# First-layer output transposed as fp16 halves, and W1 in three bf16 parts

## The chip, the core and the metric

The kernel runs on one core of one Trainium2 chip. The time is that of the device for one execution, in microseconds (us), and the median over several executions is compared. A profile of one execution shows what each engine does: TensorE (PE in the profile, with weight loads as PEld), VectorE (DVE), ScalarE (ACT), GpSimd (POOL) and SyncE (SP). Matrix products land in PSUM, everything else lies in SBUF. Here GpSimd has two tasks: it does some additions, and it issues the DMA transfers that load the adjacency.

## What is computed

Two layers of a graph network on 4096 nodes with 64 features. The adjacency matrix is 4096 x 4096 of zeros and ones, held as float32.

```python
# layer 0: weights decay with the rank of a neighbour in its row
support = x @ W0
mask = (adj != 0)
rank = cumsum(mask, axis=1); deg = rank[:, -1:]
k = minimum(deg, 100); pos = rank - (deg - k)
w = mask * where(pos > 0, 0.5 ** (k - pos), 0)
x1 = layernorm(x + w @ support + b0)

# layer 1: mean over neighbours and the node itself
deg = clip(sum(adj, axis=1) + 1, 1)
h = (adj @ x1 + x1) / deg
z = concat([x1, h]) @ W1 + b1
z = relu(z); z = z / max(norm(z), 1e-12)
out = layernorm(x1 + z)
```

The change is in the part of layer 1 that doesn't need `adj @ x1`. Multiplied by deg, z becomes deg * (x1 @ W1a + b1) + x1 @ W1b + (adj @ x1) @ W1b, where W1a is the upper and W1b the lower half of W1. The kernel computes all but the last term ahead, and calls it c1. The factor deg drops out when z is divided by its norm.

## The kernel before

The transposed adjacency is cut into 8 slabs g of 512 target nodes (R), and each slab into 8 tiles k of 512 source nodes. A tile is loaded by one DMA from GpSimd's queue (`load_next`, L109), is cast from float32 to bf16 on the way, and takes one of 23 buffers. The 64 pairs (g, k) are the 64 steps of the main loop, in the order of slabs and, within a slab, from k = 7 down to 0. Six loads are issued ahead of the loop; step i then issues load number 6+i (counted from 0) after GpSimd's other work of that step.

A step has these parts, in TensorE's order: `count` (L237) counts the neighbours of tiles that come next, in groups that are called chunks (of one tile in slab 0, two in slabs 1 to 3, four after that). In the first step of a chunk of two or four, the tiles of the next chunk are counted in pairs, and in a chunk of four a second pair two steps later. `spread` (L255) turns the counts of a whole chunk into ranks. `weigh` (L270, L280) makes the exponents of the weights of this step's tile in two PSUM buffers, which ACT (L287) and DVE (L288) turn into weights w. `some_sums` (L307) does up to four early products of layer 1 with tiles that are still in SBUF. `gather` (L298) multiplies the weights of the step before with x.

A slab's first layer ends in the steps after its last tile. With i = 8(g+1), hooks put this work on each engine: i+1 the sum and the product with W0 (`first_hT`, `first_pz`), i+2 the addition of x and the moments, i+4 the normalized x1 (L422), i+5 its fp16 high half (`first_hi`, ACT, L427) and what that leaves (`first_xl`, DVE, L431), i+6 the low half (`first_lo`, ACT, L434), scaled by 2048. The halves stand side by side in x1hl. They are the stationary operand of all products adj @ x1.

c1 is made by a second line of work in the same steps. `first_px` (i+5, L439) transposes x1 in float32, four blocks of 128 nodes. `first_x1T` (i+6, ACT, L442) copies that to SBUF, over a row of ones. `first_pu` (i+6, L447) multiplies it by W1 in float32; the bias b1 is W1's 65th row. `first_c1` (i+8, DVE, L453 and L454) multiplies one half by deg and adds the other.

What fixes the order: each engine works through its own instructions as the program lists them. Within a step of the loop GpSimd's hooks come ahead of `load_next`, and DVE's hooks come at the end of the step. GpSimd's hooks in the loop are the split of x (`split_x`, slab 0 only), the load of x for a slab (`load_x`, at 8g+3) and the addition of b0 to it (`add_b0`, L227, at 8g+7). A load waits until the tile that had its buffer is no longer needed, that is until its sums are done or until ACT has copied it to fp8 (`keep_next`, L320), and until the transfer eight issues ahead of it in GpSimd's queue has landed. The PSUM buffers named "m" are two, and count, rank, transpose and product take turns in them. `ready` says from which step on a tile may be used for early sums: from the step in which the x1hl of its source nodes is written.

After the 64 steps a last stage, written out by hand, does the rest of adj @ x1 slab by slab (`own`), with the last slab's first layer between, and then the output.

Of the kernel before, what the change touches and what calls it, by code (L numbers as in the profile page):

```python
# [9 lines left out]
F32 = mybir.dt.float32  # L10
BF16 = mybir.dt.bfloat16
FP16 = mybir.dt.float16
# [4 lines left out]
ALU = mybir.AluOpType  # L17
AX = mybir.AxisListType
PE = mybir.EngineType.PE
ACT = mybir.EngineType.Activation  # L20
DVE = mybir.EngineType.DVE
POOL = mybir.EngineType.Pool
SP = mybir.EngineType.SP

P = 128
R = 512
TB = R // P
# [5 lines left out]
LO = 2048.0  # L33
# [7 lines left out]
def adj_resnorm_kernel(  # L41
# [26 lines left out]
    nc = tc.nc  # L68
    D = w0.shape[0]
    NG, NK = adjT.shape[0], adjT.shape[1]  # L70
# [5 lines left out]
    const = ctx.enter_context(tc.tile_pool(name="const", bufs=1))  # L76
# [8 lines left out]
    ps_m = ctx.enter_context(tc.tile_pool(name="ps_m", bufs=2, space=PSUM))  # L85
# [9 lines left out]
    when = {s: i for i, s in enumerate(steps)}  # L95
# [17 lines left out]
    x1 = const.tile([P, NB, D], F32, name="x1")  # L113
    xhl = const.tile([P, NB, 2 * D], FP16, name="xhl")
    x1hl = const.tile([P, NB, 2 * D], FP16, name="x1hl")
    c1 = const.tile([P, NB, D], F32, name="c1")
# [36 lines left out]
    ident = const.tile([P, P], F32, name="ident")  # L153
# [29 lines left out]

    w0_sb = const.tile([P, D], F32, name="w0_sb")
    wn_sb = const.tile([P, D], F32, name="wn_sb")
    w1_sb = const.tile([D + 1, 2 * D], F32, name="w1_sb")
    b0_sb = const.tile([P, D], F32, name="b0_sb")
    part = {}
    deg = const.tile([P, NB], F32, name="deg")
    least = const.tile([P, NB], F32, name="least")  # L190
    x1T = const.tile([D + 1, R], F32, name="x1T")
    nc.vector.memset(x1T[D : D + 1, :], 1.0)

    def load_weights():
        nc.sync.dma_start(out=w0_sb[0:D, :], in_=w0)
        nc.sync.dma_start(out=w0_sb[D:P, :], in_=w0)
        nc.sync.dma_start(out=b0_sb, in_=b0.partition_broadcast(P))
        nc.sync.dma_start(out=w1_sb[0:D, 0:D], in_=w1[0:D, :])
        nc.sync.dma_start(out=w1_sb[0:D, D : 2 * D], in_=w1[D : 2 * D, :])
        nc.sync.dma_start(out=w1_sb[D : D + 1, 0:D], in_=b1[None, :])  # L200
        nc.sync.dma_start(out=wn_sb[0:D, :], in_=w1[D : 2 * D, :])
        nc.sync.dma_start(out=wn_sb[D:P, :], in_=w1[D : 2 * D, :])

# [12 lines left out]
    def prepare():  # L216
        nc.vector.tensor_scalar(w0_sb[0:D, :], w0_sb[0:D, :], 2.0**W_EXP, None, ALU.mult)
        nc.vector.tensor_scalar(w0_sb[D:P, :], w0_sb[D:P, :], 2.0**W_EXP / LO, None, ALU.mult)
        nc.vector.memset(w1_sb[D : D + 1, D : 2 * D], 0.0)

    def prepare_last():
        nc.vector.tensor_scalar(wn_sb[D:P, :], wn_sb[D:P, :], 1.0 / LO, None, ALU.mult)

    def add_b0(g):

        xs = x1[:, ts(g, TB), :]
        nc.gpsimd.tensor_tensor(xs, xs, b0_sb.unsqueeze(1).to_broadcast([P, TB, D]), ALU.add)  # L227
# [78 lines left out]
    def second(acc, g, b, first, last):  # L306
        nc.tensor.matmul(acc, lhsT=x1hl[:, b, :], rhs=A[g][b // KB][:, b % KB, :], start=first, stop=last)  # L307
# [23 lines left out]

    def ready(i, g, b):
        k = b // KB
        return i >= NK * (k + 1) + 6 and i >= when[g, k]

    def evict_part(g):
        acc = acc1.pop(g)
# [6 lines left out]
    def some_sums(i, n):  # L344

        done = None
        while n and todo and done is None and ready(i, todo[0][0], todo[0][1]):
            g, b, first, last = todo.pop(0)
            if first:
                acc1[g] = ps_a.tile([P, R], F32, tag="acc1", name=f"acc_part_{g}_{b}")  # L350
            second(acc1[g], g, b, first, last)
            have[g] = b // KB + 1
            n -= 1
            if last:
                done = g
        return done


    ep = {}
# [74 lines left out]
        nc.scalar.mul(x1hl[:, ts(g, TB), D : 2 * D], ep["xl", g], LO)  # L434

    def first_px(g):
        px = ep["px", g] = ps_m.tile([D, R], F32, tag="m", name=f"px_{g}")
        for t in range(TB):
            nc.tensor.transpose(px[:, ts(t, P)], x1[:, g * TB + t, :], ident)  # L439

    def first_x1T(g):
        nc.scalar.copy(x1T[0:D, :], ep["px", g])  # L442

    def first_pu(g):
        pu = ep["pu", g] = ps_m.tile([P, TB, 2 * D], F32, tag="m", name=f"pu_{g}")
        for t in range(TB):
            nc.tensor.matmul(pu[:, t, :], lhsT=x1T[:, ts(t, P)], rhs=w1_sb, start=True, stop=True)  # L447

    def first_c1(g):

        pu = ep["pu", g]
        t1 = epi.tile([P, TB, D], F32, tag="sq", name=f"t1_{g}")
        nc.vector.tensor_tensor(t1, pu[:, :, 0:D], deg[:, ts(g, TB)].unsqueeze(2).to_broadcast([P, TB, D]), ALU.mult)  # L453
        nc.vector.tensor_tensor(c1[:, ts(g, TB), :], pu[:, :, D : 2 * D], t1, ALU.add)  # L454

    hooks = defaultdict(list)

    def at(i, engine, fn, *args):
        hooks[i, engine].append((fn, args))
# [5 lines left out]
    for k in range(NK):  # L465
        i = when[0, k]
        at(i, POOL, split_x, k)
        at(i, DVE, split_x_low, k)
    at(NK - 2, DVE, prepare)
    at(2 * NK + 2, DVE, prepare_last)  # L470
    for g in range(NG):
        at(NK * g + 3, POOL, load_x, g)
        at(NK * g + 7, POOL, add_b0, g)
    for g in range(NG - 1):
        i = NK * (g + 1)
        at(i + 1, ACT, first_hT, g)
        at(i + 1, PE, first_pz, g)

        at(i + 2, DVE, first_y, g)
        at(i + 2, DVE, first_mv, g)  # L480
        at(i + 3, "ACT, late", first_s, g)
        at(i + 4, DVE, first_r, g)
        at(i + 4, DVE, first_x1, g)
        at(i + 5, ACT, first_hi, g)
        at(i + 5, DVE, first_xl, g)
        at(i + 5, PE, first_px, g)
        at(i + 6, ACT, first_lo, g)
        at(i + 6, ACT, first_x1T, g)
        at(i + 6, PE, first_pu, g)
        at(i + 6, DVE, first_least, g)  # L490
        at(i + 8, DVE, first_c1, g)


# [9 lines left out]

    nc.vector.memset(w0_sb, 0.0)
    load_weights()
    spread(0, NK - 1)
    held = None
    for c, chunk in enumerate(chunks):
        ahead = chunks[c + 1] if c + 1 < len(chunks) else []
        n, m = len(chunk), len(ahead)  # L510
# [5 lines left out]
        for (g, k), share in zip(chunk, shares):  # L516
            i = when[g, k]
# [26 lines left out]
    L = NG - 1  # L544
# [3 lines left out]
    def own(g, b0, b1):  # L548

        for b in range(b0, b1):  # L550
            second(acc[g], g, b, b == have[g] * KB, b == NB - 1)
# [136 lines left out]
    first_least(L)  # L688
    own(5, 24, last)
    own(2, 16, last)  # L690
    first_px(L)
    first_x1T(L)
    own(0, 16, 24)
    own(5, last, NB)
    last_hT(5)
    own(2, last, NB)
    last_hT(2)
    first_pu(L)
    first_c1(L)

    u = unit(5, 2)
# [117 lines left out]
```

## Time and profile before

| | us |
|---|---|
| median of 3 executions | 272.93 |
| lowest and highest | 272.83, 273.19 |
| execution that was profiled | 273.33 |
| its span, from first to last instruction | 271.5 |

Some groups of the profile of this execution, in the work that the change touches. A float32 matmul appears as two passes in the trace where it has 128 rows or columns of products, so L447 has 64 records for 32 products.

| line, engine | what | count | mean ns of one |
|---|---|---|---|
| L439 PE | transpose of x1, float32, 128 columns | 32 | 273 |
| L447 PE | product with W1, float32, 128 columns | 64 | 275 |
| L442 ACT | copy of x1T, 64 x 512 | 8 | 567 |
| L453 DVE | deg times one half | 8 | 416 |
| L454 DVE | sum of both | 8 | 425 |
| L109 POOL | issue of a load of the adjacency | 65 | 548 |

A matmul's duration in the trace includes its way through the array; the distance from one start to the next is what TensorE's time is made of. It is 109 ns for L439 and 111 ns for L447.

How to read the profile: each engine has a share of busy time. For TensorE this says little of how near it is to its peak. The page also cuts the span in 40 slices and gives the busy share of each in tenths. The chain of waits follows back, from the last instruction, what each one waited for. A wait is shown behind an instruction in brackets: how long its engine stood idle, and what ended it.

### The profile page before, as it was taken

The page shows a single profiled execution, that of the slowest core. Times are in us where ns is not written, and L with a number is a line of the kernel's source. Part 1 is how long each engine was busy: PE and PEld are TensorE (multiplying, and loading weights), DVE is VectorE, ACT ScalarE, POOL GpSimd, SP SyncE. Part 2 cuts the span into 40 slices and gives each one's busy share as a digit, 9 for nine tenths or more (in the row PEclk, how much of TensorE's full clock was granted, in tenths as well). Part 3 has the DMA queues.
Part 4 walks back from the last instruction along what each step waited for, and adds up shares of the span by engine and source line. Part 5 has one row for each costly group of instructions (what it writes and reads, how often), then busy time and mean ns, then how long its engine had stood idle before and what let it go on. Part 6 is the DMA issues. An engine that isn't in the chain of part 4 may idle for free.

```text
span 271.5 us, 4838 instructions
## 1 busy us (share of the span) xinstructions
PE 237.3 (87%) x1865; PEld 105.0 (39%) x1865; DVE 176.3 (65%) x480; ACT 157.9 (58%) x226; POOL 61.9 (23%) x111
## 2 busy tenths in 40 slices
PE   8397688979899999999899999999998999997820
PEld 2122124334434343443344344434343546555710
DVE  5566634875596778367846684576577456597884
ACT  4456627897798869768854463436545322146351
POOL 8565551231101320322122121210200000221100
PEclk9979959999999999999999999999999999999985
DMA  6999999999997999799999999990500000010010
GB/s 97 195 230 234 241 212 214 222 214 214 223 214 141 165 211 214 124 171 214 182 179 205 203 162 180 168 168 12 98 2 0 0 2 0 0 42 20 19 58 21
DMA packets 12072, 37.13 MB, mean 137 GB/s; under 512 B 2066, under 2 KB 3218, under 8 KB 12050
## 3 DMA queue, kind: packets, MB, share of 16 engines
q0 software_dynamic: 10128, 35.66, 68.1%
q1 hardware_dynamic: 1922, 1.18, 1.5%
q8 instruction: 14, 0.23, 0.3%
q14 instruction: 8, 0.07, 0.1%
HBM read 69.34 MB, written 1.05 MB: 259 GB/s over the span
## 4 chain that ended last, share of the span: by engine, by line
PE 51%; DVE 11%; ACT 8%; issue 3%; POOL 1%; DVEq 0%; POOLq 0%; ACTq 0%
PE acc L298 10%; PE acc_part L307 9%; PE v L270 8%; PE v L280 5%; ACT w L287 4%; PE acc_right L307 3%; DVE w L288 3%; PE cnt L237 3%; PE vb L307 3%; PE pu L447 2%; PE va L307 2%; PE pz L594 2%; PE pz L395 2%; DVE x L422 1%; ACT a L320 1%
## 5 line engine op out<-in xcount | busy, mean ns | idle before, releaser
L288 DVE TENSOR_SCALAR w<-v 128x1024 int16<-128x1024 f32 x64 | 78.2, 1222 | 45.3 <-PE v L280 45.2
L287 ACT ACTIVATE w<-v,less 128x1024 int16<-128x1024 f32 x64 | 71.3, 1114 | 56.9 <-PE v L280 39.9
L298 PE MATMUL acc<-w,xhl 128*128 128x512 bf16 x256 | 67.2, 385 | 2.4 <-ACT hT L389 2.1
L109 POOL DMA_DIRECT2D a<-in_adjT_dram x65 | 35.5, 548 | 122.1 <-PE acc_part L307 49.9
L270 PE MATMUL v<-a,tri 64*64 64x512 bf16 x512 | 42.0, 397 | 4.3 <-ACT w L287 2.6
L298 PEld LDWEIGHTS <-xhl 128*128 128x128 f16 x256 | 23.9, 99 | 32.5 <-issue 9.5
L320 ACT CAST a<-a 128x1024 fp8e4<-128x1024 bf16 x32 | 33.3, 1039 | 0.0
L307 PEld LDWEIGHTS <-x1hl 128*128 128x128 f16 x224 | 19.8, 98 | 27.0 <-issue 5.7
L307 PE MATMUL acc_part<-a,x1hl 128*128 128x512 bf16 x108 | 28.0, 381 | 1.8 <-ACT x1hl L434 1.3
L247 DVE TENSOR_TENSOR cs<-cnt,cs 128x512 bf16<-128x512 f32 x20 | 13.8, 691 | 20.5 <-PE cnt L237 20.4
L237 PE MATMUL cnt<-a,pick 128*32 128x512 bf16 x256 | 21.9, 399 | 6.0 <-DMA a<-in_adjT_dram 6.0
L280 PE MATMUL v<-near,mine 32*128 32x512 bf16 x256 | 25.7, 391 | 0.2 <-ACT near L257 0.2
L270 PEld LDWEIGHTS <-tri 64*64 64x64 bf16 x512 | 12.6, 106 | 30.2 <-issue 28.0
L257 ACT ACTIVATE near<-rep,most 128x512 bf16<-128x512 f32 x28 | 19.1, 682 | 3.8 <-PE rep L255 3.7
L633 POOL TENSOR_TENSOR y<-y,x 128x256 f32<-128x256 f32 x7 | 5.0, 726 | 56.1 <-DVE y L630 56.1
L280 PEld LDWEIGHTS <-mine 32*128 32x128 bf16 x256 | 6.5, 91 | 24.9 <-issue 24.9
L255 PE MATMUL rep<-cs,further 128*128 128x512 bf16 x28 | 11.2, 400 | 3.7 <-DVE cs L247 1.7
L307 PE MATMUL acc_right<-a,x1hl 128*128 128x512 fp8e4 (+1 forms) x56 | 12.7, 379 | 0.0
L237 PEld LDWEIGHTS <-pick 128*32 128x32 bf16 x256 | 4.6, 94 | 19.8 <-issue 11.5
L655 ACT ACTIVATE o<-y,off,r_l 128x64 f32<-128x64 f32 x28 | 9.7, 428 | 3.1 <-issue 1.7
L382 DVE BATCH_NORM_STATS2 st_l<-y 128x6 f32<-128x64 f32 x60 | 9.0, 214 | 0.7 <-POOL y L633 0.6
L427 ACT CAST x1hl<-x 128x256 f16<-128x256 f32 x8 | 3.2, 406 | 10.1 <-DVE x L422 10.1
(139 smaller groups left out, 238.6 us busy)
## 6 DMA issues: line engine op xcount, KB each, us to landing
a<-in_adjT_dram POOLq DMA_DIRECT2D x63, 512.0 KB, 9.7
c<-in_x_pairs_dram POOLq DMA_DIRECT2D x8, 128.0 KB, 11.6
x<-in_x_dram POOLq DMA_DIRECT2D x8, 128.0 KB, 7.9
out_dram<-o SPq DMA_DIRECT2D x7, 128.0 KB, 1.7
a<-in_adjT_dram POOLq DMA_DIRECT2D x2, 256.0 KB, 4.7
out_dram<-o_7a SPq DMA_DIRECT2D x1, 64.0 KB, 1.9
out_dram<-o_7b SPq DMA_DIRECT2D x1, 64.0 KB, 1.5
w_sb<-in_L_gnn_weight_dram SPq DMA_DIRECT2D x2, 16.0 KB, 6.5
```

The source lines that it names most:

```text
L109: nc.gpsimd.dma_start(out=a[:, qs, :], in_=adjT[g, k][:, qs, :])
L237: nc.tensor.matmul(cnt[g][q * 32 : (q + 1) * 32, :], lhsT=pick[:, PW - 2 * k : PW - 2 * k + 32], rhs=A[g][k][:, q, :], start=first, stop=last,
L247: nc.vector.tensor_tensor(new, cnt[g], cs[g], ALU.add)
L255: nc.tensor.matmul(pr, lhsT=further, rhs=cs[g], start=True, stop=True)
L257: nc.scalar.activation(near[g], pr, AF.Relu, bias=most, scale=-1.0)
L270: nc.tensor.matmul(v[i][halves[c], r, :], lhsT=tri[halves[r], :], rhs=A[g][k][halves[r], 2 * i + c, :], start=True, stop=False,)
L280: nc.tensor.matmul(v[i][:, r, :], lhsT=mine[rows, 2 * k : 2 * k + 2, :], rhs=nr[rows, :], start=False, stop=True,)
L287: nc.scalar.activation(w[:, 0:2, :], v[0], AF.Relu, bias=less)
L288: nc.vector.tensor_scalar(w[:, 2:4, :], v[1], -STEP * MAX_NEIGH, 0.0, ALU.add, ALU.max)
L298: nc.tensor.matmul(acc0[g], lhsT=xhl[:, b, :], rhs=w[:, q, :].bitcast(BF16), start=(k, q) == (NK - 1, 0), stop=(k, q) == (0, KB - 1),)
L307: nc.tensor.matmul(acc, lhsT=x1hl[:, b, :], rhs=A[g][b // KB][:, b % KB, :], start=first, stop=last)
L320: nc.scalar.copy(kept[g, k][:, qs, :], A[g][k][:, qs, :], saturate=False)
```

## The change

x1 is no longer transposed in float32. The two fp16 halves in x1hl, 128 columns for each node, are transposed instead, so x1T is 128 x 512 in fp16: rows 0 to 63 the high half, rows 64 to 127 the low half times 2048. W1 stands twice below itself, the lower copy divided by 2048, so that one product takes both halves. W1 is cut into three bf16 parts whose sum is W1, and each block of nodes is multiplied by the three, into one sum in PSUM. The 65th row is gone; deg * b1 is now made by GpSimd (`first_b1`), which also adds it to the rest (in `first_c1`).

The steps move too. `first_px` goes from i+5 to i+6 and `first_x1T` and `first_pu` go from i+6 to i+7; early sums (`ready`) wait for one more step. `prepare_last`, with the making of the three parts, goes from step 18 to step 7. In the last stage four products of slab 0 come ahead of `first_px`.

```diff
-    w1_sb = const.tile([D + 1, 2 * D], F32, name="w1_sb")
+    w1_sb = const.tile([P, 2 * D], F32, name="w1_sb")
+    w1_parts = const.tile([P, 3, 2 * D], BF16, name="w1_parts")
+    b1_sb = const.tile([P, D], F32, name="b1_sb")
...
-    x1T = const.tile([D + 1, R], F32, name="x1T")
-    nc.vector.memset(x1T[D : D + 1, :], 1.0)
+    x1T = const.tile([P, R], FP16, name="x1T")
+    ident16 = const.tile([P, P], FP16, name="ident16")
+    nc.vector.tensor_copy(ident16, ident)
...
-        nc.sync.dma_start(out=w1_sb[0:D, 0:D], in_=w1[0:D, :])
-        nc.sync.dma_start(out=w1_sb[0:D, D : 2 * D], in_=w1[D : 2 * D, :])
-        nc.sync.dma_start(out=w1_sb[D : D + 1, 0:D], in_=b1[None, :])
+        for h in range(2):
+            for c in range(2):
+                nc.sync.dma_start(out=w1_sb[h * D : (h + 1) * D, c * D : (c + 1) * D], in_=w1[c * D : (c + 1) * D, :])
+        nc.sync.dma_start(out=b1_sb, in_=b1.partition_broadcast(P))
...
-        nc.vector.memset(w1_sb[D : D + 1, D : 2 * D], 0.0)
...
         nc.vector.tensor_scalar(wn_sb[D:P, :], wn_sb[D:P, :], 1.0 / LO, None, ALU.mult)
+        nc.vector.tensor_scalar(w1_sb[D:P, :], w1_sb[D:P, :], 1.0 / LO, None, ALU.mult)
+        for j in range(3):
+            nc.vector.tensor_copy(w1_parts[:, j, :], w1_sb)
+            if j < 2:
+                nc.vector.tensor_tensor(w1_sb, w1_sb, w1_parts[:, j, :], ALU.subtract)
...
-        return i >= NK * (k + 1) + 6 and i >= when[g, k]
+        return i >= NK * (k + 1) + 7 and i >= when[g, k]
...
-        px = ep["px", g] = ps_m.tile([D, R], F32, tag="m", name=f"px_{g}")
+        px = ep["px", g] = ps_m.tile([P, R], FP16, tag="m", name=f"px_{g}")
         for t in range(TB):
-            nc.tensor.transpose(px[:, ts(t, P)], x1[:, g * TB + t, :], ident)
+            nc.tensor.transpose(px[:, ts(t, P)], x1hl[:, g * TB + t, :], ident16)
...
-        nc.scalar.copy(x1T[0:D, :], ep["px", g])
+        nc.scalar.copy(x1T, ep["px", g])
...
-            nc.tensor.matmul(pu[:, t, :], lhsT=x1T[:, ts(t, P)], rhs=w1_sb, start=True, stop=True)
+            for j in range(3):
+                nc.tensor.matmul(
+                    pu[:, t, :], lhsT=x1T[:, ts(t, P)], rhs=w1_parts[:, j, :], start=j == 0, stop=j == 2
+                )
+
+    def first_b1(g):
+
+        nc.gpsimd.tensor_tensor(
+            c1[:, ts(g, TB), :],
+            deg[:, ts(g, TB)].unsqueeze(2).to_broadcast([P, TB, D]),
+            b1_sb.unsqueeze(1).to_broadcast([P, TB, D]),
+            ALU.mult,
+        )
...
-        nc.vector.tensor_tensor(c1[:, ts(g, TB), :], pu[:, :, D : 2 * D], t1, ALU.add)
+        nc.vector.tensor_tensor(t1, pu[:, :, D : 2 * D], t1, ALU.add)
+        nc.gpsimd.tensor_tensor(c, c, t1, ALU.add)
...
-    at(2 * NK + 2, DVE, prepare_last)
+    at(NK - 1, DVE, prepare_last)
...
-        at(i + 5, PE, first_px, g)
         at(i + 6, ACT, first_lo, g)
-        at(i + 6, ACT, first_x1T, g)
-        at(i + 6, PE, first_pu, g)
+        at(i + 6, PE, first_px, g)
         at(i + 6, DVE, first_least, g)
+        at(i + 7, POOL, first_b1, g)
+        at(i + 7, ACT, first_x1T, g)
+        at(i + 7, PE, first_pu, g)
         at(i + 8, DVE, first_c1, g)
...
     own(2, 16, last)
+    own(0, 16, 20)
     first_px(L)
+    first_b1(L)
     first_x1T(L)
-    own(0, 16, 24)
+    own(0, 20, 24)
```

The addition on GpSimd in `first_c1` is written in DVE's hook of step i+8, so in GpSimd's order it stands behind the load of step i+8 and ahead of that of step i+9.

## The prediction

> **What bounds the kernel now.** I read, in this order, busy shares and slices, the chain of waits, the sums of waits, and then the timelines of POOL, DVE and PE, because the change touches GpSimd, and GpSimd issues every load of the adjacency.
>
> ```profile
> PE 237.3 (87%) x1865; PEld 105.0 (39%) x1865; DVE 176.3 (65%) x480; ACT 157.9 (58%) x226; POOL 61.9 (23%) x111
> ...
> PEclk9979959999999999999999999999999999999985
> DMA  6999999999997999799999999990500000010010
> ```
>
> TensorE is the busiest engine, and the DMA engines are hardly less busy over the first 27 slices (about 183 us). Until about 40 us most counts of a tile start within 0.04 us of its landing; after that TensorE sets the pace. The chain shows this:
>
> ```profile
> 108.65 0.57 ACT x1T L442
> 109.22 0.04 issue
> 109.26 0.38 PE rep L255
> ...
> 159.03 0.44 PE px L439 x4
> ...
> 162.94 0.89 PE pu L447 x8
> ```
>
> The transposes (0.44 us a slab) and products (0.89) lie on the chain, and so, once, does the copy of x1T between them. Now GpSimd and the loads:
>
> ```profile
> 44.91 0.53 POOL L109 DMA_DIRECT2D a<-in_adjT_dram  x1 [1.91 <-DMA a<-in_adjT_dram]
> 52.46 0.72 POOL L227 TENSOR_TENSOR x<-x,b_sb 128x256 f32<-128x256 f32 x1 [7.02 <-DMA x<-in_x_dram]
> 53.13 2.17 POOL L109 DMA_DIRECT2D a<-in_adjT_dram  x4
> ...
> 108.72 0.53 POOL L109 DMA_DIRECT2D a<-in_adjT_dram  x1 [5.12 <-ACT a L320]
> ...
> 190.90 0.53 POOL L109 DMA_DIRECT2D a<-in_adjT_dram  x1 [11.30 <-PE acc_part L307]
> ```
>
> The reader is to see that GpSimd works strictly in order: an addition that waited 7.02 us for its data held four loads, which left at once when it was done. Number the tiles 0 to 63 in their order of loading; step i issues load 6+i. Load 39 is the issue at 108.72, load 63 the one at 190.90. The DMA view cut to that last issue, with nothing else under way, has its landing:
>
> ```profile
> a<-in_adjT_dram POOLq DMA_DIRECT2D x1, 512.0 KB, 5.0
> ```
>
> By the trace's semaphores loads 35, 39, 47, 55 and 63 land 3.1, 4.7, 6.5, 10.6 and 2.6 us ahead of their counting. That is all the cover there is. The timelines of DVE and PE around step 56:
>
> ```profile
> 193.40 1.22 DVE L288 TENSOR_SCALAR w<-v 128x1024 int16<-128x1024 f32 x1 [2.39 <-PE v L280]
> 194.54 0.41 DVE L453 TENSOR_TENSOR t<-pu,deg 128x256 f32<-128x256 f32 x1
> 194.99 0.42 DVE L454 TENSOR_TENSOR c<-pu,t 128x256 f32<-128x256 f32 x1
> ```
>
> ```profile
> 198.29 0.62 PE L237 MATMUL cnt<-a,pick 128*32 128x512 bf16 x8
> ```
>
> The c1 work of step 56 ends at 195.41. The last load is counted in the second half of that PE line, at 198.52.
>
> **What the Trainium skill says.** "TensorE: Matmul & The Clock Gate", Architectural detail, calls the GpSimd queue strict FIFO; the 7.02 us above agrees. "DMA: Bandwidth & Descriptors", Anatomy of one DMA (SWDGE path), gives 2.0 us fixed plus bytes over 436 GB/s. One MB read per tile makes that an estimate of 4.4 us; the trace has 5.0, which I use. TensorE, Part 1, says that the clock halves after a window of about 3.4 us without enough work. Here the clock fell after windows in which, by my count of the matmuls, TensorE streamed 9% and 27% of the time (until 13.5 and 34.0 us) and stayed after one of 39%. TensorE, Back-to-back issue gap, has 56 ns for 128 columns; the trace has 109 ns for 256 columns in bf16 (L555), half of which is 55, and 25 ns between matmuls that load 128x128 bf16 weights for one column (L397), so weight loads don't bind.
>
> **The change part by part.**
>
> Transposes and products: 4 x 109 ns = 0.44 and 8 passes x 111 = 0.89 us a slab go; 4 x 55 = 0.22 and 12 x 55 = 0.67 come. No 16-bit transpose and no bf16 product of 128 columns is in the trace; between the 25 and the 109 ns of the rows named, the 16 new ones take 0.4 to 1.7 us a slab, which is +0.9 of gain to -0.4 of loss a slab against 1.33; at 55, TensorE saves 0.44 us a slab, 3.5 in all, where it is the bound. The x1T copy keeps 512 columns (0.56).
>
> Moves by a step: px to i+6, x1T and pu to i+7, and most groups of early sums one step later (the bound 7 for 6). As many sums as before are done by the end. TensorE's waits for the low half go at 59.55 (0.30), 83.27 (0.52) and 133.71 (0.52), and those of rep for x1T at 109.26 (0.93) and 186.62 (0.14). In slabs 1, 3 and 6 the transposes stood just before a wait of TensorE for DVE's weights (81.64, 132.08, 208.63), so their removal only widens that wait. Where the transposes were hidden, the new ones (+0.22) and the shorter products (-0.22) cancel, and only a removed wait counts. So in slab 0 0.44 + 0.30 = 0.75 goes, in slab 1 0.5, in slab 2 0.44 + 0.93, in slab 3 0.5, in slab 4 0.6 (0.44 and part of the 0.32 wait for DVE's eviction at 151.16), in slab 5 0.55; in slab 6 I take 0.25, since w(63) on ACT is late next. In the tail px now needs the low half of slab 7, which ends at 221.71; four more sums carry TensorE from 219.94 to 220.80 only, so it waits 0.95 and the 0.44 is lost: +0.35 net.
>
> Start: w1_parts add about 1.3 us of DVE at step 7 (rows of 0.18 to 0.29 us), in a 1.77 us idle time before L247 at 40.46: nothing, or 0.3 if longer. The ident16 copy replaces a memset of 0.48 before a DMA-bound stretch: nothing. SP has one DMA issue more (w1 four times, b1 broadcast), some 255 packets; the hardware queue's 1922 packets took 1.5% of the span, so 0.5 us of the DMA engines' time while they are the bound. Between 0 and 0.6; I take 0.3.
>
> GpSimd: eight products (0.72 each, like L227) on a deg that is long there, nothing. Eight additions of t1 (0.72), and these wait for DVE's second c1 operation of step 8g+16, in the queue ahead of load 8g+23. Before, that load had no such wait: load 39 left at 108.72, in step 30, and now can't before step 32. DVE's order is w 1.15, t 0.45, c 0.42; then the addition 0.77 with its semaphore, the issue, and 5.0 us: the load lands 7.85 us after w(8g+16) starts. It is counted two steps later in slabs 2 to 5: 5.47, 5.62, 5.47 and 5.12 us after that w. So TensorE stops for 2.4, 2.2, 2.4 and 2.7 us. All of it is exposed, since the counts stand ahead of the weighing in TensorE's order.
>
> The loads behind follow at 2.45 us in a full queue and up to 3.8 after an empty one or beside a load of x; I take 2.9 for the next and 3.5 with x. In slab 2 load 41 then lands 6.4 after 39 and is due 5.33 after: 1.1 more (0.3 to 2.1). In slab 4, 0.2; slab 3, nothing. In slab 1 load 31 itself is in time, but 32 to 35, with x between, land by 19.2 us after w(24), and load 35 is due 16.85 after (16.5, plus a group of sums that now falls in between, 0.86, less the transposes): 2.35 (0.8 to 3.6). In slab 0 the margin is 0.9: nothing, or 0.5.
>
> The sum, as shifts against before, w(i) being the start of DVE's weights of step i. Start and slab 0: w(16) -0.45. Slab 1's 0.5 and the group of sums that moves behind w(24): -1.8, thus 88.75. Load 35 is counted 19.2 later, at 107.95 for 107.06: +0.9. Without the x1T wait (0.93) w(32) is at 0.0. Load 39 adds 2.4, load 41 1.1: +3.5. Slab 3's 0.5: +3.0; load 47: +5.2. Slab 4's 0.6: +4.6; loads 55 and 57: +7.2. Slab 5's 0.55: +6.65; load 63: +9.35. Slab 6 -0.25, small waits for w that the stops cover -0.2, tail +0.35: +9.25. That is 13.35 of stops less 4.1 of gains. The span of 271.5 becomes 280.8. The execution profiled took 273.33 with what lies around its span, so 282.6 for it; the median of the runs shown is 0.4 below: 282.2.
>
> **The rivals.**
>
> The hold is harmless: the change is then worth its gains alone, 4.1 less the 0.2 that only the stops cover, 273.33 - 3.9 - 0.4 = 269.0 us. For it: loads land 4 to 14 us early through most of the middle. Against: the holding load is exactly the one whose cover disappears, and the wait is in the program's order. This is the rival on the faster side; it decides if the stops of TensorE together stay below 3.9 us of the 13.35.
>
> The hold bites in part: landings 1 us quicker, or less TensorE work saved between w and the count, 272.5 to 277.5: 13.35 less some 7. Against: no load of 512 KB lands within less than 5.0 us.
>
> The clock joins in: a stop of 2.4 us wholly inside one window of 3.4 leaves some 26% work, about where the clock fell at 34.0. Each time costs a window at half speed, 1.7 us. One to four of these: 283.9 to 289. Against: a stop must fall wholly in one window, for about a third of the positions.
>
> **How the numbers follow.** The forecast, 277.5 to 285, has a chance of 0.62; the clock beyond that 0.14; the hold in part 0.12; the hold harmless 0.12. The range that leaves 2 in 10 out is 275 to 287.5; the likeliest case's own is 277.5 to 285. A difference under 0.2%, 0.5 us, can't be told from none here. Faster 0.13, same 0.02, slower 0.85.
>
> **What would show it.** Right: POOL's loads 39, 47, 55 and 63 directly after an addition that waited for DVE's t; TensorE's counts (and their weight loads) waiting for the adjacency some 2 to 3 us a slab from slab 1 on, in place of 6.0 us in all before and none after 40 us; px at 55 ns, pu at 55. Wrong: no waits of the counts for DMA after 50 us, or landings well under 5 us after such an issue, or time lost in DVE or ACT in place of this.

## The result, and the profile after

| | before | after |
|---|---|---|
| median, us | 273.06 | 291.26 |
| lowest and highest | 272.83, 273.31 | 291.1, 291.8 |
| ratio | | 1.067 [1.0651, 1.0688] |
| span of the profiled execution | 271.5 | 289.4 |
| mean granted TensorE clock | 0.965 | 0.942 |

The change makes the kernel 18.2 us slower. The page of the profile after, TensorE's and GpSimd's shares and the slices of the clock, the DMA engines and what they moved:

```profile
PE 237.6 (82%) x1866; PEld 103.2 (36%) x1897; DVE 178.1 (62%) x485; ACT 158.2 (55%) x226; POOL 72.3 (25%) x127
...
PEclk9989989999999995998998999989999999999985
DMA  6999999994998999079919991799240000000111
GB/s 105 192 231 236 230 215 215 220 216 67 188 213 161 167 211 212 10 146 206 214 36 164 201 213 25 127 198 216 60 93 0 0 2 0 2 5 32 36 38 36
```

Where the DMA line was an almost unbroken row of nines before, it now has holes: 67, 10, 36, 25 and 60 GB/s, one for each of five slabs, and from the second on some 29 us (four slices of 7.2) apart. Three of the clock's dips (slices 19, 22 and 27) come one or two slices after a hole; the deepest (slice 16) comes six after the first. The sums of waits, us in total, times, and the longest, first before and then after:

```profile
POOL a L109 <- PE acc_part L307: 49.9, 16, 11.3
...
PE cnt L237 <- DMA a<-in_adjT_dram: 6.0, 7, 2.7
```

```profile
POOL c L476 <- DVE t L475: 86.5, 7, 18.2
...
PE cnt L246 <- DMA a<-in_adjT_dram: 22.3, 14, 3.1
...
POOL a L109 <- PE acc_part L316: 13.6, 5, 5.8
```

GpSimd now spends up to 18.2 us in one wait, for DVE's part of c1. Its waits for a buffer behind early sums shrink from 49.9 us to 13.6: the addition that waits comes first. TensorE's counts wait 22.3 us for the adjacency in place of 6.0. The load that stands directly behind the waiting addition is called the held one below, and the wait itself the hold.

One slab in detail, slab 2. GpSimd's timeline, with load 39 as the first of the two at 123.37 (before: 108.72):

```profile
103.33 1.13 POOL L109 DMA_DIRECT2D a<-in_adjT_dram  x2
122.70 0.72 POOL L476 TENSOR_TENSOR c<-c,t 128x256 f32<-128x256 f32 x1 [18.24 <-DVE t L475]
123.37 1.10 POOL L109 DMA_DIRECT2D a<-in_adjT_dram  x2
124.46 0.56 POOL L123 DMA_DIRECT2D x<-in_x_dram  x1
124.99 2.14 POOL L109 DMA_DIRECT2D a<-in_adjT_dram  x4
```

The chain of waits through the same place (start, length, what):

```profile
120.53 1.23 DVE w L297
121.76 0.34 DVE t L474
...
122.12 0.44 DVE t L475
...
122.70 0.67 POOL c L476
123.37 5.09 DMA a<-in_adjT_dram
128.47 0.04 issue
128.51 0.40 PE cnt L246 x4
```

From DVE's weights to the count it is 7.98 us; before, TensorE came to this count 5.47 us after the same weights. The difference, 2.5 us, is about the 2.33 that TensorE then stands still (a stop), and it repeats. TensorE's timeline at the last load, which stands for the line at 198.29 shown of before:

```profile
213.47 0.40 PE L246 MATMUL cnt<-a,pick 128*32 128x512 bf16 x4
216.16 0.40 PE L246 MATMUL cnt<-a,pick 128*32 128x512 bf16 x4 [2.28 <-DMA a<-in_adjT_dram]
```

The two tiles of a pair were one group of eight matmuls; now the second waits 2.28 us for its landing. All stops after 45 us, by the load that was late: load 25 1.27, load 34 0.14, load 35 3.11, load 39 2.33, load 47 2.23, load 55 2.40, load 63 2.28. They sum to 13.76.

The clock is the second loss. TensorE's busy time in seven stretches, with the clock granted in each (start and end, length, busy, clock, DMA share, GB/s):

```profile
105.60:109.00 3.40, 1.59 (x15) 1.00 1.07 216
109.00:115.84 6.84, 5.17 (x32) 0.50 1.07 214
126.10:129.50 3.40, 1.07 (x20) 1.00 1.06 210
129.50:132.90 3.40, 3.18 (x11) 0.50 1.06 201
132.90:153.00 20.10, 18.74 (x166) 1.00 0.71 139
184.10:187.50 3.40, 1.00 (x19) 1.00 1.06 212
187.50:190.90 3.40, 3.40 (x18) 0.50 1.08 190
```

In the traces every stretch at half clock inside the run lasts 3.41 us or a multiple of it; such a piece of time is called a window here. Four times after 45 us a window with a stop in it is followed by one or two at half the clock (half windows), five in all or 17.07 us.

The new multiplication itself does what it should: transposes and products start 56 ns apart at the full clock, where 55 was reckoned.

### The profile page after: what moved, and what is told of

Read it like the earlier page. It is cut to its first block, busy times and chain, and to the rows that moved or that the text cites. A ratio compares the mean times of both kernels' runs of the same rounds, so it can differ in the third digit from the quotient of the medians.

```text
span 289.4 us, 4893 instructions
## 1 busy us (share of the span) xinstructions
PE 237.6 (82%) x1866; PEld 103.2 (36%) x1897; DVE 178.1 (62%) x485; ACT 158.2 (55%) x226; POOL 72.3 (25%) x127
## 4 chain that ended last, share of the span: by engine, by line
PE 40%; DMA 27%; DVE 15%; ACT 7%; issue 5%; POOL 4%; ACTq 0%; DVEq 0%; POOLq 0%
DMA a<-in_adjT_dram 23%; PE v L279 8%; PE acc L307 7%; PE acc_part L316 5%; DVE w L297 5%; PE v L289 4%; DMA c<-in_x_pairs_dram 4%; ACT w L296 3%; PE cnt L246 3%; PE acc_right L316 3%; PE pu L457 2%; PE pz L617 2%; PE va L316 2%; PE vb L316 1%; POOL a L109 1%
## 5 line engine op out<-in xcount | busy, mean ns | idle before, releaser
L307 PE MATMUL acc<-w,xhl 128*128 128x512 bf16 x239 | 65.7, 391 | 2.7 <-issue 1.1
L279 PE MATMUL v<-a,tri 64*64 64x512 bf16 x512 | 42.9, 405 | 5.4 <-ACT w L296 2.8
L246 PE MATMUL cnt<-a,pick 128*32 128x512 bf16 x256 | 22.8, 394 | 22.4 <-DMA a<-in_adjT_dram 22.3
L307 PEld LDWEIGHTS <-xhl 128*128 128x128 f16 x256 | 24.6, 101 | 31.3 <-issue 9.5
L476 POOL TENSOR_TENSOR c<-c,t 128x256 f32<-128x256 f32 x8 | 5.8, 722 | 99.7 <-DVE t L475 86.5
L289 PE MATMUL v<-near,mine 32*128 32x512 bf16 x256 | 26.5, 404 | 0.2 <-ACT near L266 0.2
L246 PEld LDWEIGHTS <-pick 128*32 128x32 bf16 x256 | 5.2, 94 | 37.0 <-issue 27.3
L264 PE MATMUL rep<-cs,further 128*128 128x512 bf16 x28 | 12.0, 427 | 2.6 <-DVE cs L256 1.6
L236 POOL TENSOR_TENSOR x<-x,b_sb 128x256 f32<-128x256 f32 x8 | 5.8, 725 | 25.7 <-DMA x<-in_x_dram 25.7
```

The source lines that it names most:

```text
L246: nc.tensor.matmul(cnt[g][q * 32 : (q + 1) * 32, :], lhsT=pick[:, PW - 2 * k : PW - 2 * k + 32], rhs=A[g][k][:, q, :], start=first, stop=last,
L264: nc.tensor.matmul(pr, lhsT=further, rhs=cs[g], start=True, stop=True)
L279: nc.tensor.matmul(v[i][halves[c], r, :], lhsT=tri[halves[r], :], rhs=A[g][k][halves[r], 2 * i + c, :], start=True, stop=False,)
L289: nc.tensor.matmul(v[i][:, r, :], lhsT=mine[rows, 2 * k : 2 * k + 2, :], rhs=nr[rows, :], start=False, stop=True,)
L307: nc.tensor.matmul(acc0[g], lhsT=xhl[:, b, :], rhs=w[:, q, :].bitcast(BF16), start=(k, q) == (NK - 1, 0), stop=(k, q) == (0, KB - 1),)
```

## The experiments

All ratios are to runs of the kernel before on the same chip in the same series.

**Without the hold.** Two ways to take the wait out of GpSimd's queue, and leave the rest of the change.

```diff
-        nc.gpsimd.tensor_tensor(c, c, t1, ALU.add)
+        nc.vector.tensor_tensor(c, c, t1, ALU.add)
```

> The changed kernel with one edit: the last addition of c1 is made by DVE, so nothing on GpSimd waits for DVE ahead of a load; the product deg*b1 stays on GpSimd. If the hold of the loads (with the stops of TensorE and the half clock after them) is the cause of the loss: 268 to 271 us, no waits of the counts for DMA after 50 us. If the moved steps, the new products or GpSimd's extra work are the cause: 285 us or more. DVE's eight extra additions (about 0.4 us each) may take up to 2 us back.

Measured: 270.03 us, ratio 0.988 [0.987, 0.990]. The waits of its GpSimd and of its counts:

```profile
POOL a L109 <- PE acc_part L316: 46.9, 19, 7.7
...
PE cnt L246 <- DMA a<-in_adjT_dram: 6.2, 6, 2.7
```

Loads wait for buffers again, as before (49.9), and the counts' waits are back at 6.2, none after 50 us. This one instruction on GpSimd carries the whole loss and more: with it on DVE, the change gains 3.1 us.

```diff
-        nc.gpsimd.tensor_tensor(c, c, t1, ALU.add)
+    def first_c1_add(g):
+        nc.gpsimd.tensor_tensor(c1[:, ts(g, TB), :], c1[:, ts(g, TB), :], ep["t1", g], ALU.add)
...
+        if g < NG - 2:
+            at(i + 13, POOL, first_c1_add, g)
...
```

The additions of the last two slabs stand in the last stage.

> The changed kernel with the addition kept on GpSimd, but listed five steps later (step i+13 in place of the end of i+8), where DVE's part has long been done when GpSimd gets there. Hold as the cause: 268 to 271 us, and below the variant with DVE's addition if DVE is tight. If the time of GpSimd's additional work itself (16 operations of 0.72 us in the queue of the loads) is the cause: 285 us or more.

Measured: 270.23 us, ratio 0.990 [0.988, 0.992]. All of GpSimd's additional work is still there, so its own time is not the cause; only its place is. DVE's eight extra additions in the variant above cost nothing that can be seen beside this one.

**The hold alone.** The kernel before, with a copy on GpSimd in the place of the addition.

```diff
-        nc.vector.tensor_tensor(c1[:, ts(g, TB), :], pu[:, :, D : 2 * D], t1, ALU.add)
+        nc.vector.tensor_tensor(t1, pu[:, :, D : 2 * D], t1, ALU.add)
+        nc.gpsimd.tensor_copy(c1[:, ts(g, TB), :], t1)
```

> The kernel before with only the hold: DVE writes the sum of c1 to t1 and GpSimd copies it to c1 in the same place of its queue where the changed kernel adds. Hold as the cause: stops of 2 to 3 us in slabs 1 to 5 and the clock's fall after them, 286 to 293 us. If the hold does no harm by itself: 273 to 275 us.

Measured: 287.24, 289.95, 292.2 and 293.2 us, much more spread than the others; the two within 1.5% of the shortest are compared, and give a ratio of 1.056 [1.050, 1.063]. No other part of the change is needed for a loss of this size.

**The stops without the clock's fall.** TensorE is given products with a matrix of zeros while it would wait.

```diff
+    fill = {35: 12, 39: 9, 47: 9, 55: 9, 63: 9}
...
             for s in share:
+                for _ in range(fill.get(when[s], 0)):
+                    nc.tensor.matmul(
+                        cnt[s[0]], lhsT=zeros, rhs=A[s[0]][s[1] + 1][:, 0, :], start=False, stop=False
+                    )
                 count(*s, s == ahead[0], s == ahead[-1])
```

> The changed kernel with the hold, and with TensorE kept streaming during five of the stops: 12 (load 35) or 9 (loads 39, 47, 55, 63) products with a matrix of zeros, added to the count ahead of the tile that is waited for. They add nothing to the count. If the clock's fall after the stops is what the prediction lacked: no half clock between 45 and 270 us and 283 to 286 us. If the stops themselves are longer than they look, or something else slows the steps after them: 290 us or more.

Measured: 286.88 us, ratio 1.050 [1.048, 1.052]. Two stretches of this variant, at the same times as the first two above:

```profile
105.60:109.00 3.40, 3.19 (x24) 1.00 1.06 214
109.00:115.84 6.84, 6.10 (x54) 1.00 1.01 201
```

The clock stays at 1.00 there, and between 45 and 270 us throughout. So the fall of the clock costs 291.26 - 286.88 = 4.4 us. That is less than the 8.5 us that half speed would take from unbroken work in 17.07 us. At half speed TensorE reaches the next loads later: the filled kernel waits 3.0 us for loads 41, 43, 49 and 57, for which the changed kernel doesn't wait. With the clock up, the waits still left after 45 us sum to 6.2 us (load 49 alone 1.42, loads 41 and 43 1.3) and the 48 fillers take 48 x 216 ns = 10.4, thus 16.6 us of stops in place of 13.76. The time lies between the two expectations, 0.9 us above the first: the stops too were longer than the prediction had them.

**Fewer fillers**, 3 in each of the five stops.

```diff
-    fill = {35: 12, 39: 9, 47: 9, 55: 9, 63: 9}
+    fill = {35: 3, 39: 3, 47: 3, 55: 3, 63: 3}
```

> The changed kernel with 3 filling products in each of the five stops, 0.65 us of work in place of 1.9 to 2.6. By a count of the matmuls the clock fell after every window of 3.41 us with TensorE streaming 36% of the time or less, and stayed after every one with 37% or more. 0.65 us is 19% of a window, and the windows of the stops had 18 to 33%, so most would now be above: at most one or two half windows after 45 us and 286.5 to 288.5 us. If the clock follows the length of the stop itself, which is still some 2.3 us: four or more half windows and 290 to 292 us.

Measured: 288.15 us, ratio 1.057 [1.055, 1.059], with two half windows after 45 us in the profiled execution, after windows in which TensorE streamed 33% and 32% of the time; windows of 39% and more in its stops passed. So the clock goes with the work in a window. The length of the wait alone doesn't order the cases: in the changed kernel the wait of 2.28 us at load 63 was split over two windows with 50% and 52% of work, and no fall followed; in a run below, one of 1.69 us within a window with 36% was followed by one.

**The load of x behind the held load.**

```diff
-        at(NK * g + 3, POOL, load_x, g)
+        at(NK * g if g else 3, POOL, load_x, g)
```

on the variant with fillers, with 4 in place of 12 at load 35.

> The variant with filled stops (286.9 us), with the load of a slab's x three loads earlier, ahead of the held load, and 4 in place of 12 fillers at load 35. If the x load in the queue behind the held one is what made loads 25, 35, 41, 49 and 57 late (stops of 1.2, 3.5, 1.3, 1.4 and 0.2 us): 279.5 to 282.5 us. If they are late because a queue that starts empty is slow, whatever it holds: 285 us or more.

Measured: 281.04 us, ratio 1.030 [1.028, 1.031], 5.8 us less than with x in its old place. Loads 25, 41, 43, 49 and 57 are in time, load 35 waits 0.65. The waits after 45 us (1.9) and the 40 fillers (8.6) make 10.5 us of stops in place of 16.6, so the stops account for the gain. Without the load of x right behind the held one, the following loads are in time.

**One load later.** The wait for DVE stays, but stands behind load 8g+23.

```diff
+            at(i + 10, POOL, first_c1_add, g)
```

in place of i + 13 above.

> The changed kernel with GpSimd's addition one load later in its queue, so that the wait for DVE stays and holds load 8g+24 in place of 8g+23. If the loss depends on exactly which load is held (the one counted two steps later), the held one is now due two or more steps further on: no stops over 1 us after 50 us, 269.5 to 272 us. If any wait of GpSimd for DVE at this point harms: 284 us or more.

Measured: 272.91 us, ratio 0.999 [0.998, 1.000], 0.9 above the expected range. GpSimd's and TensorE's timelines around slab 2 show what was missed:

```profile
116.10 0.72 POOL L480 TENSOR_TENSOR c<-c,t 128x256 f32<-128x256 f32 x1 [7.75 <-DVE t L475]
116.77 0.57 POOL L109 DMA_DIRECT2D a<-in_adjT_dram  x1
117.33 0.55 POOL L123 DMA_DIRECT2D x<-in_x_dram  x1
117.87 2.13 POOL L109 DMA_DIRECT2D a<-in_adjT_dram  x4
```

```profile
126.60 0.40 PE L246 MATMUL cnt<-a,pick 128*32 128x512 bf16 x4 [1.69 <-DMA a<-in_adjT_dram]
```

Load 40, now the held one, is in time; load 41 behind it and x is not, and one half window follows at 127.72. So the expectation of no stop over 1 us failed too, and this wait still costs 2.7 us against the variant with i + 13. But one place in the queue is worth 18 us: most of the harm comes from holding a load that is due at once.

**The moves alone**, on the kernel before.

```diff
-        return i >= NK * (k + 1) + 6 and i >= when[g, k]
+        return i >= NK * (k + 1) + 7 and i >= when[g, k]
...
-        at(i + 5, PE, first_px, g)
-        at(i + 6, ACT, first_x1T, g)
-        at(i + 6, PE, first_pu, g)
+        at(i + 6, PE, first_px, g)
+        at(i + 7, ACT, first_x1T, g)
+        at(i + 7, PE, first_pu, g)
```

> The kernel before with the moves alone: float32 transposes at i+6, copy and product at i+7, early sums one step later; same products, no GpSimd addition. It splits the gain of the variant without a hold (3.1 us). If the removed waits for the low half and for the copy carry most of it: 270.5 to 271.5 us. If the cheaper products carry it: 272.5 to 273.5 us. The prediction's sums give about 1.9 us for the waits.

Measured: 271.54 us, ratio 0.994 [0.993, 0.996]. The moves bring 1.6 of the 3.1 us. The rest, about 1.5, is left by subtraction for the cheaper products with all that comes with them; no run has these alone.

**A version that beats both.** GpSimd's addition five steps later, and in the last stage:

```diff
-    own(0, 16, 20)
+    own(0, 16, 24)
     first_px(L)
...
-    own(0, 20, 24)
```

> The variant with GpSimd's addition five steps later, and in the tail all eight sums of slab 0 ahead of the transposes of the last slab, so that TensorE doesn't wait there for the low half (0.78 us in that variant). If the wait is on the path: 269.3 to 269.7 us; if the time comes back later in the tail: 270 to 270.5 us.

Measured: 269.10 us, ratio 0.986 [0.984, 0.988], 0.2 below the expected range. The wait of the last transposes for the low half is gone, and 1.1 us with it.

## Why the prediction was wrong

The direction and the mechanism were right: the held loads stopped TensorE where it was forecast. The range, 275 to 287.5, ended 3.8 us too low, and the forecast of 282.2 lacked 9.1 us. Of these the clock is 4.4, longer stops 3.3 (16.6 in the filled kernel for 13.35), and smaller gains 0.8 to 1.0; some 0.5 us stay open.

**The step that failed first: the clock was put at nothing.** The sum of the forecast has no fall of the clock. The prediction kept it as a rival with a chance of 0.14, one to four windows of 1.7 us each, because "a stop must fall wholly in one window, for about a third of the positions". Five half windows followed four of the five long stops, and they cost 4.4 us net, by the filled stops. The prediction's own third speaks against the zero: an estimate for five stops at independent positions is a chance of 0.87 for at least one fall, and one or two falls on average. Three of the stops (loads 39, 47 and 55) did lie wholly in one window, which is a matter of position. The fourth shows that they need not: at load 35 the window from 105.6 to 109.0 held only part of the stop, TensorE streamed a third of the time in it, and the clock fell for two windows. That the clock stays after 39%, as read from the trace of before, was true, but the bound lay just below, and a window with part of a stop can be under it.

**The second: what comes behind a held load.** The sum of the stops, 13.35, looks confirmed by the 13.76 measured, but the half clock had shortened some of them. With the clock up they are 16.6. The step that failed is "I take 2.9 for the next and 3.5 with x", together with the "nothing" for loads 25 and 49. Loads 24, 32, 40 and 48 landed 2.4 to 2.7 us after the one ahead, and those behind x (33, 41, 49 and 57) 4.1. The two errors nearly cancel: 6.4 us were put for both, and for loads 39 to 41 it was 6.5. So x, though it makes the loads late, was almost fully in the sum.

What was not in it are single landings a microsecond longer still: load 25 came 5.25 us after load 24, load 35 3.51 after load 34 with no x between (2.4 is usual), and in the filled kernel load 49 5.24 after load 48. At these three TensorE stopped for clearly more than was reckoned: load 25 1.27 us for nothing, load 35 3.1 to 3.3 for 2.35, load 49 1.42 for nothing in the filled kernel. The trace of before has such a landing, load 58, 5.05 us after load 57; "up to 3.8" passed over it. What makes them long stays open. In each of these four intervals a 16 KB packet of another DMA queue ("q8 instruction" on the page) passed, at 79.5 and 108.3 us for loads 25 and 35; but other such packets, at loads 46 and 50 for instance, left no mark, and no run tests it.

**The held loads themselves were right.** They were to land 7.85 us after DVE's weights and to stop TensorE for 2.4, 2.2, 2.4 and 2.7; the trace has 7.9 us for load 39 and stops of 2.33, 2.23, 2.40 and 2.28.

**The gains were a little too large.** The prediction had 3.9 us without stops; the two variants without the hold gained 3.1 and 2.9. By DVE's weights in the first of them, the start costs 0.44 for 0.3, and slab 0 brings 0.4 for 0.75. Of the waits, put at about 1.9, the moves brought 1.6. In slabs 1 and 3 TensorE now waits 0.58 for DVE's weights where it waited 0.15 before. The tail's wait for the low half was to be 0.95 and is 0.79; its removal alone brought 1.1 us. One reading was wrong without harm: the trace of before does have a bf16 product of 128 columns (L499), but a single one, so it gives no distance between starts.

**The rivals.** The harmless hold falls with the copy on GpSimd in the kernel before. Its number, 269.0, is a microsecond below where the change stands without the hold. The partial hold, with landings 1 us quicker, falls: the held loads took 5.0 to 5.2 us to land.

Not settled: how far the windows' position in time, which moves from one execution to the next, changes a single time, and what makes single landings a microsecond longer.

## What to carry to other kernels

Before an operation is handed to an engine that also issues loads, find the loads behind it in that queue and when they are due; the operation's own 0.7 us say nothing, its wait says all. Put such an operation behind the point where its input is sure to be there: here five steps later left no wait on the path, and one place in the queue made the difference between 291 and 273 us. A stop of the matrix engine of a couple of microseconds has to be priced with the slow clock after it.

## What was not expected of the hardware

The work in each window of 3.41 us can be counted from the traces: 216 ns for 512 columns, the distance between starts, the double for a float32 pass (111 ns for 128 columns in L447), and twice the time at half clock. In the 11 executions profiled, after the first 20 us, the clock fell after every window with less than 36% and after none with 37% or more (769 windows at the full clock, 33 falls); at 36% it fell once (from 124.3 us with the addition one load later) and stayed once (from 30.6 us with three fillers). A low clock stayed low after windows of 65% or less and rose after 67% or more (49 windows).

A load of x, 128 KB, between two loads of a tile put some 1.5 us on the next landing (4.1 us between landings for 2.5), where its share of the bytes, a quarter of a tile's at 2.45 us, would make 0.6. That is behind a held load. In the kernel before, two loads behind x (17 and 25) had many others ahead of them and landed 15 to 17 us after their issue; they came 2.75 us after the tile ahead, so there x took 0.3.
